# Another order inside a head group's four slots, and relative-position terms stored by blocks of 128 keys

## The chip, the cores and the metric

The kernel runs on one core of one Trainium2 chip. The metric is the device time of one execution in microseconds. Before the change it was 2924.61 us, the median of three runs (2921.96 to 2926.6).

## The reference

The input is x, 16 batches of 512 tokens with 256 features, and a conditioning vector for each batch. The block computes, all in 32-bit floats:

```
h = layernorm(x) * (1 + ca) + sa
q, k, v = h Wq + bq, h Wk + bk, h Wv + bv                 (16 heads of 16 features)
scores[l, r] = (q_l . k_r + q_l . pos[l - r] + k_r . pos[l - r]) / 4
ctx = softmax(scores) v
x = x + ga * layernorm(ctx Wo + bo + h)
h = layernorm(x) * (1 + cb) + sb
x = x + gb * (sum of the 2 of 8 experts that the router picks)
```

What matters here is the middle: each score has three terms. The one of q and k is called content. The two that use the table pos of relative distances are the q terms and the k terms.

## The kernel before

A prologue normalizes the batches and computes q, k and v, which go to DRAM (`prepare`, L261). It also brings q and k into a form in which the relative-position terms can be made by matmuls (`stationary`, L327).

The terms are made in 64 blocks. A block n covers 64 queries by 128 keys for 128 batch-heads. For one of its four parts, `q_set` (L156) runs 8 matmuls on TensorE into four PSUM banks, and ScalarE copies the four banks into an SBUF block `two[n % 2]` (L175). `k_set` (L177) runs 16 matmuls into four banks, and VectorE adds each bank to the block (L195). `store` (L199) writes a part to the DRAM tensors `rel_d`. The first ten blocks are made in the prologue (`blocks`, L375, LEAD = 10).

Then the main part works through 64 units. A unit is 128 queries of one batch, with four head groups of four heads. For a head group:

- `load_scores` (L577) brings the terms of its four heads from `rel_d` into a tile `s` of 128 x 4 x 512.
- `content` (L637) runs four 32-row matmuls into four banks. VectorE adds them to `s`, scales by 0.25 and takes each row's maximum (L650), then negates the maxima (L654).
- `exps` (L657): ScalarE's exponential of one head, in place.
- `turn` (L664): four transposes of one head's exponentials into one bank, and ScalarE's copy of it to SBUF (L671).
- `context` (L674): 16 matmuls in 32-column tiles form the weighted sum of v for the four heads, all from the copies of `turn`. It has a PSUM bank of its own.

The rest of a unit runs one unit later: `back`, `contextT`, `project` (L695 to L744), `residual` and `norm2` (L747, L756), where the reciprocal root of a variance is taken on GpSimd (L101), `modulate`, `route`, `mask_t` and `bias` (L768 to L821), and then four pairs of experts. `experts` (L823) runs two whole-array matmuls of 512 columns into one bank. `expert_sums` (L833) reads both halves of this bank: VectorE accumulates the first half (L838), ScalarE scales the second (L842), and GpSimd adds that up (L848). Term blocks run ten ahead of the units, four parts of q terms and four of k terms in a unit.

The order is written out by hand. Time is cut into slots, 16 for a unit and 4 for a head group, and `at(slot, order, fn, ...)` (L862) says in which slot and in which order a function issues its instructions; the loop at L910 calls them by slot and order. Every engine runs its own instructions in this order, and waits on semaphores for what it needs from the others. DMAs are issued by SP, in the same order.

All matmul outputs but the weighted sum come from one pool of seven PSUM banks (`bank`, L122). A matmul into a bank waits until the last reader of what the bank held is done.

In the four slots of a head group TensorE did, before the change: slot 0 a transposed head and content of the next group; slot 1 a transposed head and the weighted sum of the group before; slot 2 a transposed head, q terms and experts; slot 3 k terms and a transposed head, with the smaller pieces between. The change touches these lines:

```python
            at(q0 - 2, 7, exps, u, g, (0, 1))
            at(q0 - 1, 7, exps, u, g, (2, 3))
            at(q0 + 5, 4, context, u, g)
            at(z + 18 + 4 * pr, 6, experts, u, pr)
            at(z + 19 + 4 * pr, 1, expert_sums, u, pr)
                at(z + 2 + 4 * g, 4, rel.q_set, n, g)
                at(z + 15 + 4 * g, 2, rel.k_set, n, g)
```

## Time and profile before

| | us |
|---|---|
| median of three runs | 2924.61 |
| the profiled execution | 2935.72 |
| span of the profiled execution | 2934.0 |
| first transposed head of the first unit | 496.9 after the start |
| a unit in the steady part | 39.11 |
| TensorE, ScalarE, VectorE, GpSimd busy in the unit from 1494.0 to 1533.1 us | 39.10, 30.78, 26.41, 9.47 |
| share of the 16 DMA engines busy from 1000 to 2500 us | 0.91 |
| longest DMA entries by bytes: rel_d<-r, s<-rel_d | 256 issues of 1024 KB each, 8.5 and 7.8 us to landing |

A profile is one execution taken by the hardware profiler. Each engine's instructions have a start and a duration; for matmuls the end is modelled, so TensorE's busy time holds waits that fall between two matmuls of one group. The profiled execution is 11.1 us longer than the median of the runs.

### The profile page before, as it was taken

Reading aid. Unit: us, or ns where it says so; the run is one execution under the profiler, and the core shown is the slowest. Engines: PE = TensorE matmul, PEld = TensorE weight load, DVE = VectorE, ACT = ScalarE, POOL = GpSimd, SP = SyncE. Lnnn points to the kernel's source line nnn. Section 1 sums busy time; section 2 is a strip of 40 time slices with the busy share of each in tenths; the row PEclk is TensorE's granted clock in tenths of the full one; section 3 lists DMA queues with packets and bytes.
Section 4 is the critical chain, followed back from the end, with each engine's and each line's share of the span. In section 5 each row is a group of like instructions: output and inputs, shape, how many; then the busy total and the mean of one; then the engine's idle time right before and its main releaser. Section 6 shows DMA issues by size and latency. Waiting matters only on the chain.

```text
span 2934.0 us, 76492 instructions
## 1 busy us (share of the span) xinstructions
PE 2770.9 (94%) x30186; PEld 1803.2 (61%) x30186; DVE 1837.4 (63%) x5140; ACT 2068.8 (71%) x3938; POOL 630.1 (21%) x863
## 2 busy tenths in 40 slices
PE   8779963999999999999999999999999999999997
PEld 5556642666666666666666666666666666665654
DVE  5446542666666666666666666666666666675553
ACT  2345432877777777777777777777777777777774
POOL 1000000022222222222222222222222222223333
PEclk9989876999999999999999999999999999999998
DMA  6879998688988998899888998889899898897561
GB/s 181 306 253 317 296 299 273 223 276 283 286 282 277 294 307 279 274 285 292 281 278 286 291 289 281 278 285 288 278 286 307 279 286 281 278 278 264 201 238 43
DMA packets 855350, 796.49 MB, mean 271 GB/s; under 512 B 25545, under 2 KB 649409, under 8 KB 854737
## 3 DMA queue, kind: packets, MB, share of 16 engines
q1 hardware_dynamic: 854032, 790.03, 85.2%
q8 instruction: 240, 3.93, 0.5%
q10 hardware_dynamic: 960, 1.57, 0.2%
q14 instruction: 118, 0.96, 0.1%
HBM read 462.20 MB, written 328.25 MB: 269 GB/s over the span
## 4 chain that ended last, share of the span: by engine, by line
PE 77%; DMA 2%; POOL 2%; DVE 1%; SPq 1%; ACT 1%; issue 1%; POOLq 0%; DVEq 0%; ACTq 0%
PE pt L669 18%; PE fpy L827 15%; PE qk L644 12%; PE pq L165 10%; PE pc L684 8%; PE pk L186 8%; PE ph L732 2%; DMA vu<-v_d 1%; PE fpl L788 1%; PE pcl L699 1%; PE fpb L818 1%; PE fpt L775 1%; POOL qm L614 1%; PE pct L716 0%; POOL rstd L101 0%
## 5 line engine op out<-in xcount | busy, mean ns | idle before, releaser
L671 ACT COPY pT<-pt 128x512 f32<-128x512 f32 x1024 | 595.3, 584 | 317.9 <-PE pt L669 295.3
L195 DVE TENSOR_TENSOR r<-pk,r 128x512 f32<-128x512 f32 x1024 | 635.0, 683 | 189.2 <-PE pk L186 164.3
L660 ACT ACTIVATE s<-s,mx 128x512 f32<-128x512 f32 x1024 | 689.7, 731 | 43.3 <-DVE mx L654 39.7
L650 DVE CUSTOM_DVE_ANT_0 s<-qk,s 128x512 f32<-128x512 f32 x1024 | 644.1, 685 | 85.8 <-PE qk L644 81.4
L669 PE MATMUL pt<-ident,s 128*128 128x128 f32 x4096 | 660.0, 284 | 10.8 <-ACT s L660 10.4
L175 ACT COPY r<-pq 128x512 f32<-128x512 f32 x1024 | 525.6, 603 | 153.9 <-PE pq L165 137.1
L669 PEld LDWEIGHTS pt<-ident,s 128*128 128x128 f32 x4096 | 450.0, 143 | 284.7 <-ACT s L660 73.8
L827 PE MATMUL fpy<-we_sb,fhT 128*128 128x512 f32 x1024 | 506.1, 617 | 0.0
L848 POOL TENSOR_TENSOR ye<-ye,ye 128x256 f32<-128x256 f32 x192 | 140.5, 732 | 1597.4 <-ACT ye L842 1105.8
L838 DVE SCALAR_TENSOR_TENSOR fy<-fpy,fmask,fy 128x256 f32<-128x256 f32 x256 | 123.5, 482 | 471.6 <-PE fpy L827 319.3
L644 PE MATMUL qk<-k,qm 32*128 32x512 f32 x2048 | 380.1, 650 | 28.0 <-POOL qm L614 28.0
L186 PEld LDWEIGHTS pk<-t_f,ke 32*128 32x128 f32 x8192 | 268.3, 190 | 189.5 <-ACT r L175 124.1
L165 PE MATMUL pq<-t_r,qe 32*128 32x256 f32 x4096 | 370.5, 409 | 4.2 <-DMA qe<-eq_d 2.8
L186 PE MATMUL pk<-t_f,ke 32*128 32x128 f32 x8192 | 319.8, 287 | 8.8 <-DVE r L195 3.6
L827 PEld LDWEIGHTS fpy<-we_sb,fhT 128*128 128x128 f32 x1024 | 175.0, 190 | 195.2 <-issue 159.8
L165 PEld LDWEIGHTS pq<-t_r,qe 32*128 32x128 f32 x4096 | 240.2, 186 | 82.4 <-issue 41.7
L684 PE MATMUL pc<-pT,vu 128*32 128x128 f32 x8192 | 279.1, 277 | 0.0
L684 PEld LDWEIGHTS pc<-pT,vu 128*32 128x32 f32 x8192 | 209.9, 110 | 44.1 <-issue 43.5
L644 PEld LDWEIGHTS qk<-k,qm 32*128 32x128 f32 x2048 | 133.4, 184 | 101.5 <-DVE r L195 47.6
L101 POOL TENSOR_TENSOR rstd<-rstd,mhalf 128x1 f32<-128x1 f32 (+1 forms) x144 | 87.9, 610 | 436.0 <-DVE rstd L100 428.1
L842 ACT ACTIVATE ye<-fpy,fmask 128x256 f32<-128x256 f32 x256 | 125.3, 490 | 51.3 <-DVE fy L838 51.3
L614 POOL TENSOR_SCALAR qm<-qs,par 128x256 f32<-128x256 f32 x128 | 117.7, 932 | 150.1 <-DMA k<-k_d 137.8
(110 smaller groups left out, 2061.7 us busy)
## 6 DMA issues: line engine op xcount, KB each, us to landing
rel_d<-r SPq DMA_DIRECT2D x256, 1024.0 KB, 8.5
s<-rel_d SPq DMA_DIRECT2D x256, 1024.0 KB, 7.8
vu<-v_d SPq DMA_DIRECT2D x64, 576.0 KB, 7.5
ke<-ek_d SPq DMA_DIRECT2D x128, 256.0 KB, 7.2
k<-k_d SPq DMA_DIRECT2D x128, 256.0 KB, 6.6
gt<-gates_d SPq DMA_DIRECT2D x64, 256.0 KB, 4.7
v_d<-v SPq DMA_DIRECT2D x16, 576.0 KB, 6.4
xt<-in_x SPq DMA_DIRECT2D x16, 512.0 KB, 5.9
```

The costliest lines, as they stand in the source:

```text
L165: nc.tensor.matmul(bs[t][:, a * 256 : (a + 1) * 256], e[32 * t : 32 * t + 32, (g % 2) * 2 + a, :], t_r[32 * t : 32 * t + 32, :, m0 : m0 + RK],
L175: nc.scalar.copy(dst[:, t], bs[t].rearrange("p (a c) -> p a c", a=2))
L186: nc.tensor.matmul(bs[t][:, a * 128 : (a + 1) * 128], e[32 * t : 32 * t + 32, a, :], t_f[32 * t : 32 * t + 32, :, m0 : m0 + LQ], start=Tru ...
L195: nc.vector.tensor_tensor(dst, bs[t].rearrange("p (r l) -> p l r", r=8), dst, ALU.add)
L614: nc.gpsimd.tensor_scalar(qm[:, pa], qs, par[:, pa : pa + 1], None, ALU.mult)
L644: nc.tensor.matmul(bs[t], t_["q"][rows, pa, cc, :], t_["k", cc][rows, :], start=True, stop=True)
L650: nc.vector.tensor_tensor_reduce(st[:, t, :], bs[t], st[:, t, :], 0.25, -3.0e38, ALU.add, ALU.max, mx[:, t : t + 1],)
L660: nc.scalar.activation(t_["s", g][:, t, :], t_["s", g][:, t, :], AF.Exp, bias=t_["m", g][:, t : t + 1])
L669: nc.tensor.transpose(pt[:, cols], t_["s", g][:, t, cols], ident)
L671: nc.scalar.copy(pT, pt)
L684: nc.tensor.matmul(pc[32 * t : 32 * t + 32, g, :], t_["v"][:, rb, h * VW : h * VW + 32], pTs[t][:, rb * P : (rb + 1) * P], start=(rb == 0) ...
L827: nc.tensor.matmul(py, t_["hT"][:, kc, :], we_sb[:, kc, pr * 2 * E : (pr + 1) * 2 * E], start=(kc == 0), stop=(kc == NE - 1),)
```

## The change

In a head group the weighted sum is issued one slot earlier and so stands directly before content of the next group. Experts stay in their slot but now stand before the q terms. The sums over the experts (VectorE and ScalarE) move from the head of the following slot to directly behind the experts. Of the four exponentials one is issued in slot 2 and three in slot 3, where it was two and two. Q terms are copied in two halves: banks 0 and 1 directly after the matmuls, banks 2 and 3 in the next slot, after that slot's transposed head, which now stands before the k terms. `bias` is issued one slot later.

The DRAM tensors of the terms change their layout from (batch-head, query, 512 keys) to (batch-head, block of 128 keys, query, 128 keys). What a store writes for one head is now one contiguous piece of 16 x 128 numbers. A load reads pieces of 128 numbers, and is four DMAs, one for each head.

```diff
-    rel_d = [dram.tile([P, P, S], F32, tag=f"rel_{n}", name=f"rel_d{n}") for n in range(8)]
+    rel_d = [dram.tile([P, NL, P, RK], F32, tag=f"rel_{n}", name=f"rel_d{n}") for n in range(8)]
...
+            self.banks = bs
+            self.q_copy(n, g, (0, 1))
+
+        def q_copy(self, n, g, ts):
             dst = self.two[n % 2][:, 16 * g : 16 * g + 16, :].rearrange(
                 "p (a t i) r -> p t a (i r)", a=2, t=4
             )
-            for t in range(4):
-                nc.scalar.copy(dst[:, t], bs[t].rearrange("p (a c) -> p a c", a=2))
+            for t in ts:
+                nc.scalar.copy(dst[:, t], self.banks[t].rearrange("p (a c) -> p a c", a=2))
...
-                out=rel_d[s * 4 + lb][:, l0 : l0 + 16, rb * RK : (rb + 1) * RK],
+                out=rel_d[s * 4 + lb][:, rb, l0 : l0 + 16, :],
...
                 rel.q_set(n, g)
+                rel.q_copy(n, g, (2, 3))
...
-        nc.sync.dma_start(
-            out=st, in_=rel_d[s * 4 + lb][h0 : h0 + 7 : 2].rearrange("h l r -> l h r")
-        )
+        for t in range(4):
+            nc.sync.dma_start(
+                out=st[:, t, :].rearrange("p (rb r) -> p rb r", r=RK),
+                in_=rel_d[s * 4 + lb][h0 + 2 * t].rearrange("rb l r -> l rb r"),
+            )
...
-            at(q0 - 2, 7, exps, u, g, (0, 1))
-            at(q0 - 1, 7, exps, u, g, (2, 3))
+            at(q0 - 2, 6.3, exps, u, g, (0,))
+            at(q0 - 1, 5, exps, u, g, (1, 2, 3))
             for t in range(4):
                 at(q0 + t, 3, turn, u, g, t)
-            at(q0 + 5, 4, context, u, g)
+            at(q0 + 4, 4, context, u, g)
...
-        at(z + 16, 7, bias, u)
+        at(z + 17, 6, bias, u)
         for pr in range(4):
             at(z + 18 + 4 * pr, 6, experts, u, pr)
-            at(z + 19 + 4 * pr, 1, expert_sums, u, pr)
+            at(z + 18 + 4 * pr, 6.6, expert_sums, u, pr)
...
-                at(z + 2 + 4 * g, 4, rel.q_set, n, g)
-                at(z + 15 + 4 * g, 2, rel.k_set, n, g)
+                at(z + 2 + 4 * g, 7, rel.q_set, n, g)
+                at(z + 3 + 4 * g, 3.5, rel.q_copy, n, g, (2, 3))
+                at(z + 15 + 4 * g, 4, rel.k_set, n, g)
```

## The prediction

> **What bounds the kernel now.** I read the page first, then the busy time by stretches, then the timelines of TensorE, ScalarE and VectorE over one unit, then the waits.

> ```profile
> span 2934.0 us, 76492 instructions
> PE 2770.9 (94%) x30186; PEld 1803.2 (61%) x30186; DVE 1837.4 (63%) x5140; ACT 2068.8 (71%) x3938; POOL 630.1 (21%) x863
> ...
> PE   8779963999999999999999999999999999999997
> ...
> DMA  6879998688988998899888998889899898897561
> ```

> TensorE looks full from 600 us to the end, and a unit (16 slots, 4 head groups) takes 39.11 us from its first transpose to that of the next unit (1494.03 to 1533.15 us), every unit alike. But ends of matmuls are modelled, so a wait inside a group of matmuls counts as busy. I therefore read starts, from one group to the next. Timeline of TensorE in the third head group of a unit (start, duration, what):

> ```profile
> 1488.36 2.02 PE L165 MATMUL pq<-t_r,qe 32*128 32x256 f32 x16
> 1490.30 1.98 PE L827 MATMUL fpy<-we_sb,fhT 128*128 128x512 f32 x4
> 1492.21 1.17 PE L186 MATMUL pk<-t_f,ke 32*128 32x128 f32 x32
> 1493.32 0.66 PE L669 MATMUL pt<-ident,s 128*128 128x128 f32 x4
> ```

> The q terms take 1.94 us here, and 1.08 in another group of the same unit; 0.87 us of it is a wait for a PSUM bank. In the four groups of the unit from 1494 us the q terms take 1.08, 1.15, 1.26 and 1.95, and content 1.84, 0.96, 1.62 and 1.07 (0.96 where a 32-row matmul follows, 1.07 where a transpose does). So waits are 1.13 us in q terms and 1.32 in content: 2.45 of 39.11 us. The waits name who held the banks (window 800 to 2800 us):

> ```profile
> PEld qk L644 <- DVE r L195: 41.9, 187, 0.3
> ...
> ACT ye L842 <- DVE fy L838: 17.5, 26, 1.7
> ...
> PEld pq L165 <- DVE mx L650: 14.7, 46, 0.3
> ```

> Content waits for VectorE's adds on the k terms, q terms for its maxima over content. The totals are small because most of such a wait hides in a busy matmul; the pairs are what matters. The middle line matters below: ScalarE's half of an expert pair (L842) waits for VectorE's half (L838). The same third group on ScalarE and VectorE:

> ```profile
> 1489.99 2.05 ACT L175 COPY r<-pq 128x512 f32<-128x512 f32 x4 [0.89 <-PE pq L165]
> 1491.91 1.36 ACT L660 ACTIVATE s<-s,mx 128x512 f32<-128x512 f32 x2
> 1493.14 0.49 ACT L842 ACTIVATE ye<-fpy,fmask 128x256 f32<-128x256 f32 x1
> ```

> ```profile
> 1489.84 0.42 DVE L654 TENSOR_SCALAR mx<-mx 128x4 f32<-128x4 f32 x1
> 1490.17 0.41 DVE L760 BATCH_NORM_STATS2 stats<-x 128x6 f32<-128x256 f32 x1
> ...
> 1492.17 0.41 DVE L765 TENSOR_SCALAR xn<-x,mv,rstd 128x256 f32<-128x256 f32 x1 [1.18 <-POOL rstd L101]
> 1492.50 0.48 DVE L838 SCALAR_TENSOR_TENSOR fy<-fpy,fmask,fy 128x256 f32<-128x256 f32 x1
> ```

> In this group VectorE runs the second layer norm between the maxima and its expert half: 2.66 us from L654 to L838, of which 1.18 wait for GpSimd. Before the change that hurts nobody: ScalarE has made its four q copies and two exponentials before it comes to L842.

> [...] four transposes take 0.436 us between whole-array work and 0.530 ahead of tiled matmuls (0.094 more), and the first of the four expert matmuls takes 0.533 to the next start after q terms where the others take 0.429 (0.104 more). [...] Here, packets of 512 bytes took 29 ns on average, of 2048 bytes 97, of 8192 bytes 319.

> **The change, part by part.**

> *Weighted sum beside content, experts beside q terms.* Whole-array and tiled work alternate three times a group instead of four: 0.094 + 0.104 = 0.198 us a group, 0.79 a unit[...]. Also the sum (1.01 us) now stands between k terms and content, and experts (1.81) between content and q terms, which covers the 2.45 us of waits. At most 3.24 us a unit are to be gained.

> *ScalarE's new queue.* Its order in a group becomes: three transposed copies, exponential 0, L842, q copies 0 and 1, fourth transposed copy, q copies 2 and 3, exponentials 1 to 3. Now L842 stands ahead of the q copies. By the banks that the built program hands out, the third and fourth k-term banks are those of q copies 0 and 1, and one transpose group (0.59 us) stands between q terms and k terms.

> - Ordinary group, q terms ending at T: L842 is done about T + 0.14, the copies start 0.48 apart and last 0.59, so the second is out at T + 1.21, and 0.05 goes to the semaphore. The k terms go round their four banks, so nearly all of their 1.1 us follows: end T + 2.32. Without a wait it is T + 0.59 + 1.10 = T + 1.69. Added: 0.63, three times 1.9.
> - Third group, counted from the end of the second group's k terms: adds from 0.1, four by 0.60, then the first norm's statistics and L750 until 4.3; maxima 4 by 0.61, so L654 at 6.9; 2.66 on, L838: 9.5 to 10.0; L842 to 10.5; copies 0 and 1 out at 11.6; k terms end at 12.7. TensorE alone: projection 1.17, transposes 0.53, sum 1.01, content 1.2, transposes 0.93, experts 1.81, q terms 1.28 (0.2 of them a wait), transposes 0.59, k terms 1.10: 9.6. Added: 3.1, and the 0.2.
> - What is late next: ScalarE does exponentials 1 to 3 (0.61 each) only after the q copies, and small copies behind them hold banks that content takes. In the first group the mask's copy ends 4.68 after T, content would start at T + 4.13: 0.5. In the fourth the modulated copies end 1.1 after content could use them: 1.1.

> Sum of the unit: 39.11 − 2.45 − 0.79 + 1.9 + 3.3 + 1.6 = 42.67, so 42.6 us, +3.5. The same reckoning with the old order gives 39.2 against the 39.11 measured, so its steps are sound to some 0.1 where they can be tested.

> *The last ten units* have no q or k terms. The weighted sum there follows the fourth transposes with only one transpose group between, and that fourth copy stands behind L842: 0.5 to 0.9 us a group, less what runs hidden; I take +3 a unit (0 to 4.5).

> *Terms by 128 keys.* A store turns from 2048 packets of 512 bytes into 128 of 8192: 2048·29/16 = 3.7 us of the 16 DMA engines becomes 128·319/16 = 2.6. A load turns from 512 of 2048 bytes into 2048 of 512: 3.1 becomes 3.7. Four of each a unit: −2.0 us of some 36. In the steady part that is worth nothing, TensorE covers it. Loads are four DMAs instead of one: 12 more a unit at about 0.45 us on SP, 5.4 us. SP has room:

> ```profile
> SPq L203 <- DVE r L195: 442.6, 43, 11.2
> ```

> that is 10 us a unit in which the store at the head of SP's queue waited for VectorE (window 800 to 2500 us). A load is still issued eight slots, near 20 us, ahead of its content, and lands in 7.8; should that cover go, a load late by x costs x. In the prologue DMA is the bound from 350 to 490 us (share 0.83 to 1.09 in most stretches); 16 stores fall there, 16·1.1 = 18 us less transfer, not all on the path. I take −15 (0 to −40).

> Total: 2934.0 + 54·3.5 + 10·3 − 15 = 3138 us of span. The profiled execution took 2935.7, the median 2924.6 is 11.1 below: 3138 + 1.7 − 11.1 = **3129 us**.

> **Rivals.**

> *Cover works, queue does not bite* (not slower): all waits go and no new one comes: 2934.0 − 54·3.24 − 15 = 2744, so 2735 us. For it: the new neighbours do cover VectorE's work, and ScalarE has idle time (30.8 of 39.1 us busy). Against: the chain L765, L838, L842, copies, k terms. It decides once new waits stay below 3.24 us a unit, which needs L842 not to hold the copies in the third group.

> *Only the short wait* (about the same or faster): the third group costs 0.63 like the others and content waits stay at 0.5: 39.11 − 3.24 + 2.5 + 0.5 = 38.9 a unit, 2934 − 11 − 15, so 2899 us. For it: GpSimd may answer sooner. Against: 1.18 us waited in every unit of before.

> *Transfers become the bound* (slower): if reads of 512 bytes cost 40 ns, not 29, the loads take 20.5 us a unit, transfers near 39.5 and late loads show: with the queue's wait hidden behind that, 40 to 44 us a unit, near 3100 us. Against: 512-byte packets averaged 29 ns at a 0.91 share.

> **How the numbers follow.** The main case has 0.80, cover works 0.07, only the short wait 0.06, transfers 0.07. The main case by itself spans 3050 to 3200 (±1.2 us a unit, ±15 at the two ends); to leave no more than 2 in 10 out I reach down towards smaller third-group waits, 3010. A measurement of this kernel tells 0.2% from no change. Faster 0.12, same 0.01, slower 0.87.

> **What would show it.** Right: k terms at 1.7 us in three groups and above 3.5 in the third; L842 idle before it, released by L838; q terms near 1.08; content near 1.07 in the second and third groups; the unit at 42 to 43 us; the first weighted sum some 10 to 20 us earlier. Wrong: k terms at 1.10 in every group, or loads of s named as what content waits for.

## The result: 10% slower, and the profile after

The changed kernel takes 3217.6 us (median of four runs, 3202.4 to 3232.5), the kernel before 2925.6 in the same session: a ratio of 1.100, interval 1.094 to 1.105. The forecast was 3129 us, range 3010 to 3200. The direction and the place of the loss were as forecast; a tenth was lost where the sum had 7%.

The profiled execution took 3202.4 us, 1.7 of it outside the span. From the page of the changed kernel, its head, and two rows of the span in 40 slices (TensorE's busy tenths and the clock it was granted):

```profile
span 3200.7 us, 78389 instructions
...
PE 2955.9 (92%) x30186; PEld 1919.0 (60%) x30186; DVE 1841.2 (58%) x5140; ACT 2058.1 (64%) x3938; POOL 628.8 (20%) x863
...
PE   8789749999999999999999999999999999998887
...
PEclk9899859999999999999999999999999999999987
DMA  6977987878887878877778887788877778886661
```

VectorE and ScalarE are busy for about as long as before (1837 and 2069 us), and TensorE issues exactly as many instructions. No engine has more to do. TensorE's 185 us more of busy time are waits inside its matmul groups, and a slower clock, as the following views show. The DMA row is lower than before, and between 800 and 2500 us no TensorE instruction waits for a load of `s`.

The start of `contextT`'s transposes, one pair per unit, marks each unit; from one to the next is an interval, and the intervals divide the span without a gap. All numbers are of the two profiled executions:

| stretch | before, us | after, us | difference, us | forecast, us |
|---|---|---|---|---|
| start to the first of them | 541.3 | 522.8 | −18.5 | −15 |
| 53 intervals in the steady part | 2068.3 | 2309.3 | +241.0 | +189 |
| the ten intervals after | 290.0 | 333.0 | +43.0 | +30 |
| rest | 34.4 | 35.6 | +1.2 | 0 |

Before, every steady unit takes 39.11 us. After, one in five takes 42.80 us and nearly all others 43.90. The 42.80 is close to the forecast (42.6). The extra 1.1 us in four of five units was not in it.

The steps of the forecast are seen best in the third head group of a unit. Timeline of TensorE, changed kernel (start, duration, what, the wait before it in brackets; line numbers are those of the changed kernel: 4 higher than before for the k terms and the q copies, 7 higher behind them):

```profile
1489.44 1.88 PE L834 MATMUL fpy<-we_sb,fhT 128*128 128x512 f32 x4
1491.25 1.48 PE L165 MATMUL pq<-t_r,qe 32*128 32x256 f32 x16
1492.66 0.66 PE L676 MATMUL pt<-ident,s 128*128 128x128 f32 x4
1493.25 0.48 PE L190 MATMUL pk<-t_f,ke 32*128 32x128 f32 x2
1495.31 2.96 PE L190 MATMUL pk<-t_f,ke 32*128 32x128 f32 x30 [1.58 <-ACT ye L849]
1498.20 0.69 PE L782 MATMUL fpt<-ident,xn 128*128 128x128 f32 x2
```

Two of 32 matmul instructions of the k terms go out, then TensorE stands still until ScalarE's expert half (L849) is done. From start to start the group takes 4.95 us, where before it took 1.10. In a unit of 42.80 us it takes 4.09. The same stretch on ScalarE, and then on VectorE:

```profile
1491.79 0.72 ACT L667 ACTIVATE s<-s,mx 128x512 f32<-128x512 f32 x1 [1.46 <-DVE mx L661]
1494.78 0.47 ACT L849 ACTIVATE ye<-fpy,fmask 128x256 f32<-128x256 f32 x1 [2.27 <-DVE fy L845]
1495.15 1.06 ACT L179 COPY r<-pq 128x512 f32<-128x512 f32 x2
```

```profile
1491.58 0.17 DVE L661 TENSOR_SCALAR mx<-mx 128x4 f32<-128x4 f32 x1
1491.66 0.42 DVE L767 BATCH_NORM_STATS2 stats<-x 128x6 f32<-128x256 f32 x1
...
1493.94 0.41 DVE L772 TENSOR_SCALAR xn<-x,mv,rstd 128x256 f32<-128x256 f32 x1 [1.46 <-POOL rstd L101]
1494.27 0.48 DVE L845 SCALAR_TENSOR_TENSOR fy<-fpy,fmask,fy 128x256 f32<-128x256 f32 x1
```

This is the forecast chain, link by link: maxima, second norm with its wait for GpSimd, VectorE's expert half (L845), ScalarE's half (L849), and only then the q copies (L179), which start at 1495.15 us, 0.37 after L849, though the q terms end at 1492.73. From L661 to L845 it is 2.69 us, forecast 2.66. The k terms wait first for L849 itself, because one of their four banks is that of the expert pair, then for the q copies.

The waits of the changed kernel (800 to 2800 us; us in total, times, longest):

```profile
ACT ye L849 <- DVE fy L845: 190.9, 137, 2.3
...
PEld pk L190 <- ACT ye L849: 79.4, 46, 1.8
PE pk L190 <- ACT ye L849: 70.5, 45, 1.6
...
PEld pk L190 <- ACT r L179: 50.8, 265, 0.2
```

The first row was 17.5 us before, and the second and third rows did not exist. The two expert halves read the same bank; why ScalarE's waits for VectorE's was not shown.

What the forecast did not have is in the busy time by stretches. The columns are the stretch, then busy us and instructions of PE, PEld, DVE, ACT, POOL, then the granted clock, the DMA share and GB/s. The first row is from a unit of 42.80 us, the others from the next, right after the wait:

```profile
1451.00:1453.00 2.00, 0.51 (x3) 0.33 (x3) 0.81 (x2) 1.03 (x3) 0.57 (x2) 1.00 0.01 3
...
1496.00:1498.00 2.00, 2.00 (x28) 1.77 (x27) 0.11 (x1) 2.00 (x5) 0.06 (x1) 0.60 0.00 0
1498.00:1500.00 2.00, 2.00 (x20) 1.48 (x22) 2.00 (x4) 2.00 (x5) 0.00 (x0) 0.55 0.02 4
1500.00:1502.00 2.00, 2.00 (x42) 1.04 (x31) 0.51 (x2) 0.70 (x2) 0.00 (x0) 1.00 0.50 193
```

After the wait TensorE runs at half its clock from 1496.38 us for 3.41 us, then at full speed again. The 53 steady intervals hold 42 such stretches. Before, the clock stays at 1.00 from 525 us to 2655 us.

### The profile page after: what moved, and what is told of

Its sections match the earlier page's. It is cut to its first block, busy times and chain, and to the rows that moved or that the text cites. A ratio compares the mean times of both kernels' runs of the same rounds, so it can differ in the third digit from the quotient of the medians.

```text
span 3200.7 us, 78389 instructions
## 1 busy us (share of the span) xinstructions
PE 2955.9 (92%) x30186; PEld 1919.0 (60%) x30186; DVE 1841.2 (58%) x5140; ACT 2058.1 (64%) x3938; POOL 628.8 (20%) x863
## 3 DMA queue, kind: packets, MB, share of 16 engines
q10 hardware_dynamic: 960, 1.57, 0.1%
## 4 chain that ended last, share of the span: by engine, by line
PE 42%; POOL 10%; DMA 9%; issue 8%; DVE 6%; SPq 6%; ACT 5%; POOLq 0%; DVEq 0%; ACTq 0%
PE pk L190 8%; PE pt L676 8%; PE fpy L834 6%; PE qk L651 6%; PE pc L691 6%; SPq L588 4%; POOL qm L621 4%; PE pq L165 3%; DVE s L657 3%; DMA s<-rel_d 3%; DMA k<-k_d 2%; POOL rstd L101 2%; DMA rel_d<-r 2%; ACT s L667 2%; POOL x L760 1%
## 5 line engine op out<-in xcount | busy, mean ns | idle before, releaser
L676 PEld LDWEIGHTS pt<-ident,s 128*128 128x128 f32 x4096 | 472.1, 146 | 321.5 <-issue 170.3
L190 PE MATMUL pk<-t_f,ke 32*128 32x128 f32 x8192 | 530.1, 302 | 88.4 <-ACT ye L849 81.5
L179 ACT COPY r<-pq 128x512 f32<-128x512 f32 x1024 | 551.8, 608 | 40.1 <-PE pq L165 23.3
L190 PEld LDWEIGHTS pk<-t_f,ke 32*128 32x128 f32 x8192 | 406.8, 194 | 213.5 <-ACT ye L849 91.7
L651 PE MATMUL qk<-k,qm 32*128 32x512 f32 x2048 | 352.0, 664 | 23.2 <-DMA s<-rel_d 23.0
L165 PE MATMUL pq<-t_r,qe 32*128 32x256 f32 x4096 | 336.1, 406 | 4.2 <-DMA qe<-eq_d 2.9
L165 PEld LDWEIGHTS pq<-t_r,qe 32*128 32x128 f32 x4096 | 216.0, 186 | 195.6 <-issue 46.8
L691 PE MATMUL pc<-pT,vu 128*32 128x128 f32 x8192 | 317.0, 295 | 5.3 <-ACT pT L678 5.3
L849 ACT ACTIVATE ye<-fpy,fmask 128x256 f32<-128x256 f32 x256 | 121.4, 474 | 285.3 <-DVE fy L845 281.2
L691 PEld LDWEIGHTS pc<-pT,vu 128*32 128x32 f32 x8192 | 232.6, 118 | 66.0 <-issue 48.3
L101 POOL TENSOR_TENSOR rstd<-rstd,mhalf 128x1 f32<-128x1 f32 (+1 forms) x144 | 87.8, 609 | 585.2 <-DVE rstd L100 562.7
L845 DVE SCALAR_TENSOR_TENSOR fy<-fpy,fmask,fy 128x256 f32<-128x256 f32 x256 | 123.1, 481 | 129.7 <-PE fpy L834 129.7
L651 PEld LDWEIGHTS qk<-k,qm 32*128 32x128 f32 x2048 | 102.7, 192 | 108.6 <-issue 55.7
```

What stands on the lines that cost most here:

```text
L165: nc.tensor.matmul(bs[t][:, a * 256 : (a + 1) * 256], e[32 * t : 32 * t + 32, (g % 2) * 2 + a, :], t_r[32 * t : 32 * t + 32, :, m0 : m0 + RK],
L179: nc.scalar.copy(dst[:, t], self.banks[t].rearrange("p (a c) -> p a c", a=2))
L190: nc.tensor.matmul(bs[t][:, a * 128 : (a + 1) * 128], e[32 * t : 32 * t + 32, a, :], t_f[32 * t : 32 * t + 32, :, m0 : m0 + LQ], start=Tru ...
L651: nc.tensor.matmul(bs[t], t_["q"][rows, pa, cc, :], t_["k", cc][rows, :], start=True, stop=True)
L676: nc.tensor.transpose(pt[:, cols], t_["s", g][:, t, cols], ident)
L691: nc.tensor.matmul(pc[32 * t : 32 * t + 32, g, :], t_["v"][:, rb, h * VW : h * VW + 32], pTs[t][:, rb * P : (rb + 1) * P], start=(rb == 0) ...
```

## The experiments

Each kernel ran in three timed rounds beside the kernel before, which took between 2928.8 and 2933.2 us in these sessions. Ratios are to that. The table gives the mean steady interval (51 of them) and the mean of the first nine of the last ten, from each profile.

| kernel | time, us | ratio, interval | steady, us | last, us |
|---|---|---|---|---|
| before | 2925.6 | | 39.11 | 29.6 |
| changed | 3217.6 | 1.100 (1.094 to 1.105) | 43.70 | 33.8 |
| layout only | 2917.6 | 0.996 (0.994 to 0.998) | 39.11 | 29.5 |
| order only | 3229.5 | 1.104 (1.101 to 1.107) | 43.86 | 34.0 |
| norm behind the expert half | 3042.6 | 1.039 (1.037 to 1.040) | 40.68 | 34.2 |
| third pair's matmuls twice | 3146.2 | 1.074 (1.072 to 1.076) | 42.79 | 33.6 |
| half of it twice | 3195.6 | 1.091 (1.088 to 1.093) | 43.68 | 33.5 |
| a quarter of it twice | 3196.7 | 1.091 (1.089 to 1.094) | 43.70 | 33.6 |
| weighted sum moved only | 3054.2 | 1.042 (1.040 to 1.043) | 41.04 | 31.4 |
| q copies together | 3227.2 | 1.101 (1.099 to 1.103) | 44.03 | 34.0 |
| modulated copies a slot later | 3183.9 | 1.087 (1.084 to 1.090) | 43.37 | 34.2 |
| norm behind, projection first | 3001.8 | 1.024 (1.023 to 1.026) | 40.38 | 31.0 |
| new order repaired | 2908.7 | 0.992 (0.990 to 0.994) | 39.04 | 29.1 |
| old order mended | 2865.1 | 0.977 (0.975 to 0.979) | 38.19 | 28.8 |

### The two parts of the change apart

*Layout only.* To the kernel before, the three hunks on the terms' memory layout (the tile, the store, four loads for one), nothing else.

> The order of the kernel before, with only the terms' new layout and its four loads a group. Theory (all of the loss is in the order): units stay at 39.11 us, the first weighted sum comes about 16 us earlier (16 stores of the prologue at 2.6 instead of 3.7 us of the DMA engines), so about 2910 us (2900 to 2918). Rival (512-byte reads or twelve more loads on SP's queue bind the steady part): 40 us a unit or more, 2960 us and up. Third: the layout is hidden in the prologue too, 2925 us.

Measured 2917.6 us, and 39.11 us a unit. From the page of this kernel:

```profile
span 2915.5 us, 78452 instructions
...
PE 2767.3 (95%) x30186; PEld 1801.8 (62%) x30186; DVE 1839.5 (63%) x5140; ACT 2066.4 (71%) x3938; POOL 628.7 (22%) x863
```

The span is 18.5 us shorter than before, and the first unit's `contextT` comes at 526.2 instead of 541.3 us. The gain lies in the prologue. Twelve more DMAs a unit on SP and reads of 512 bytes cost nothing in the steady part. The rival of the transfers falls.

*Order only.* The changed kernel with those three hunks undone.

> The changed order with the old layout of the terms. Theory: everything of the loss is here, units of 42.8 and 43.9 us as in the changed kernel, prologue longer by 15 to 17 us: about 3233 us (3215 to 3250). Rival (the two parts bite only together, the new loads being late in the new order): units under 41 us, below 3080 us.

Measured 3229.5 us, units of 42.8 and 43.9 us, a few of 45. The layout has no part in the loss: it is all in the order.

### The third group's wait

*Norm behind the expert half.*

```diff
-        at(z + 10, 0, norm2, u)
+        at(z + 10, 6.8, norm2, u)
```

> The changed kernel with the second layer norm on VectorE moved behind the expert half of its group. Theory (the chain xn, fy, ye, q copies, k terms of the third group, and the half-speed clock that its wait sets off): the third group's k terms 1.7 us instead of 4.1 to 4.95, no half-speed window left, unit 42.8 - 2.4 = 40.4 us, 3217.6 - 54 x 3.3 = about 3040 us (3015 to 3065). Rival A (the half-speed windows come from the other waits, or from anything else): unit about 41.3, 3217.6 - 54 x 2.4 = 3088 us. Rival B (VectorE's work is merely late elsewhere: norm2 then holds something else up): unit 42 us or more, above 3120 us.

Measured 3042.6 us. The steady unit is 40.67 us, each one alike. The k terms of the third group, on TensorE's timeline of this kernel:

```profile
1470.67 2.05 PE L190 MATMUL pk<-t_f,ke 32*128 32x128 f32 x32
1472.65 0.44 PE L782 MATMUL fpt<-ident,xn 128*128 128x128 f32 x2
```

From start to start they take 1.98 us instead of 4.09 to 4.95, and no half-speed stretch is left in the steady part. One line's place in VectorE's queue was worth 175 us. The wait's own length is 112 of them (4.09 less 1.98 us, 53 times), and 48 are the clock, as the next experiment shows; the rest is about what the changed kernel's median lies above its profiled run. The chain from the norm to the k terms stands, and rivals A and B fall; the k terms keep 0.27 us more than the 1.71 of the other groups.

*Third pair's matmuls twice.* This asks whether the clock, and not the queue, makes the other 1.1 us. More work is put where TensorE waits:

```diff
-        for kc in range(NE):
-            nc.tensor.matmul(
...
+        for _ in range(2 if pr == 2 else 1):
+            for kc in range(NE):
+                nc.tensor.matmul(
...
```

> The changed kernel with the third expert pair's four matmuls run twice into the same bank (1.72 us more of TensorE work a unit, the same result). That work falls into the time in which the third group's k terms wait. Theory (the wait starves TensorE long enough that its clock is halved for one 3.4 us window): k terms of the third group 4.09 - 1.72 = 2.4 us, no half-speed windows, all units 42.8 us, so it is faster although it does more: 3217.6 - 54 x 0.9 + 10 x (0 to 1.7) = 3170 to 3190 us. Rival A (the clock drops for another reason): units 43.7 on average as before, 3217 to 3235 us. Rival B (the expert half waits for TensorE, not for the norm): 1.7 us a unit more, about 3310 us.

Measured 3146.2 us: 71 us faster with 256 more matmul instructions. TensorE's timeline in the third group of this kernel (L850 is L849 of the changed kernel):

```profile
1472.80 1.15 PE L165 MATMUL pq<-t_r,qe 32*128 32x256 f32 x16
1473.88 0.66 PE L676 MATMUL pt<-ident,s 128*128 128x128 f32 x4
1474.46 0.48 PE L190 MATMUL pk<-t_f,ke 32*128 32x128 f32 x2
1475.13 2.12 PE L190 MATMUL pk<-t_f,ke 32*128 32x128 f32 x30 [0.18 <-ACT ye L850]
```

The wait is still there, but short: the group takes 2.71 us. Every steady unit but one of 42.93 us takes 42.77 to 42.80 us; none takes 43.9. The granted clock by stretches is 1.00 in all of 1440 to 1472 us here, two of its rows:

```profile
1460.00:1464.00 4.00, 4.00 (x45) 2.29 (x47) 1.50 (x6) 3.17 (x7) 0.73 (x1) 1.00 0.67 197
1464.00:1468.00 4.00, 4.00 (x72) 3.09 (x66) 3.25 (x7) 3.47 (x7) 0.07 (x1) 1.00 0.95 279
```

So two kernels with the same queue, and with units of the same 42.80 us when the clock is whole, differ by 47.7 us over the 53 steady intervals (2261.6 against 2309.3). The one has 42 half-speed stretches in them and the other none. That is the price of the clock, some 1.1 us for each. Of the 71 us between the medians another 5 are in the last units, and 19 lie between the medians and the profiled runs (the changed kernel's median is 15.2 us above its own, this one's 4.0 below).

*Half and a quarter of it twice.* One matmul call more on all 512 columns, or on 256:

```diff
+        if pr == 2:
+            nc.tensor.matmul(
+                py, t_["hT"][:, 0, :], we_sb[:, 0, pr * 2 * E : (pr + 1) * 2 * E],
+                start=True, stop=True,
+            )
```

> The changed kernel with half of the third expert pair's matmuls run twice (0.86 us more of TensorE work a unit instead of 1.72, the same result). The third group's k terms then take 4.09 - 0.86 = 3.2 us, a wait of 2.1 us instead of 3.0 (1.3 with the whole pair). Theory (the half-speed windows come of the length of this wait): none left or few, units of 42.8 us, about 3150 us (3140 to 3170). Rival [...]: units of 43.9 us remain, 3200 us or more.

> The same with a quarter of the pair's matmuls (0.43 us more of TensorE work, the same result): the third group's k terms take about 3.65 us, a wait of 2.55 us. Theory (length of the wait, and where it falls in the fixed raster of 3.41 us windows): half-speed windows in fewer units than 4 of 5, say 2 of 5, so about 3175 us (3150 to 3205). Rival (a threshold on the wait alone, above 2.55): none, 3147 us. Rival (below 2.55): as without it, 3200 to 3235 us.

Measured 3195.6 and 3196.7 us: both theories of mine on the length missed, and the rival that a shorter wait is enough holds, with times 3 to 4 us below what it gave. With the quarter 10 of 51 steady units take 42.8 us, with the half 13, and nearly all others 43.9 or more, as without the extra work. The 21 to 22 us that both gain are not in the steady part (43.7 us a unit as before): 5 are in the last units, and most of the rest is that the changed kernel's median lies 15 us above its profiled run. With the half, in a unit whose clock was whole during the k terms (L854 is L849 of the changed kernel):

```profile
1491.49 0.48 PE L190 MATMUL pk<-t_f,ke 32*128 32x128 f32 x2
1492.99 2.12 PE L190 MATMUL pk<-t_f,ke 32*128 32x128 f32 x30 [1.02 <-ACT ye L854]
```

The group takes 3.54 us, not 3.2: 0.33 us of the extra work went into the q terms' own wait for a bank (1.41 us there falls to 1.08). By starts, the longest stillness within the k terms is 1.82 us in the changed kernel, 1.72 with a quarter, 1.29 with the half, 0.45 with the whole pair. The first three kernels have their clock halved in most units, the last in none of the steady ones.

### The other terms of the sum

*Weighted sum moved only.* To the kernel before:

```diff
-            at(q0 + 5, 4, context, u, g)
+            at(q0 + 4, 4, context, u, g)
```

> The kernel before, with only the weighted sum moved one slot on, next to content; nothing else of the change. Theory (in the old place it stands between content and the q terms, so it covers the q terms' wait for VectorE's maxima; taken away from there the wait shows): q terms 1.9 to 2.3 us in all four groups instead of 1.08 to 1.95, content without its waits of 0.9 and 0.7 us, unit 39.11 + 1.9 = 41 us, tail units some 3 us longer: 2926 + 54 x 1.9 + 10 x 3 = about 3055 us (3030 to 3080). Rival (the neighbours save a mode change a group, nothing else moves): unit 38.7 us, 2905 us.

Measured 3054.2 us. TensorE's timeline (this kernel's lines are those of before):

```profile
1494.58 1.14 PE L644 MATMUL qk<-k,qm 32*128 32x512 f32 x8
1495.65 1.09 PE L669 MATMUL pt<-ident,s 128*128 128x128 f32 x8
1496.68 2.17 PE L165 MATMUL pq<-t_r,qe 32*128 32x256 f32 x16
```

Content takes at most 1.07 us, its waits are gone. The q terms take 2.10 to 2.49 us, and they wait for the maxima: in the waits between 800 and 2500 us, TensorE's loads for q terms behind the maxima (L650) go from 13.7 to this:

```profile
PEld pq L165 <- DVE mx L650: 106.3, 373, 0.3
```

Call cover what TensorE does between a group of matmuls and the next group that takes the same banks, while the other engines empty them. Here cover was moved from one taker of banks to another: over the unit the q terms take 9.2 us instead of 5.4, content 4.2 instead of 5.5. The change as a whole avoids this loss with the experts in front of the q terms, and then it is the k terms that stand uncovered.

*q copies together.*

```diff
-                at(z + 3 + 4 * g, 3.5, rel.q_copy, n, g, (2, 3))
+                at(z + 2 + 4 * g, 7.1, rel.q_copy, n, g, (2, 3))
```

> The changed kernel with the four q copies in one go before the fourth transposes (the halving undone). Theory (the k terms wait for q copies 0 and 1 only, which stay where they are): k terms 1.71 us in three groups and over 4 in the third as before, 3217 us within 15. Rival (the halves are what makes things late: ScalarE's two late copies hold the banks of the next content or the next q terms): two thirds of a us a group or more comes back, below 3100 us. Other way (the fourth transposed copy, now behind all four, holds up the weighted sum): 3250 us or more.

Measured 3227.2 us, no gain. Its steady units with a whole clock take 42.75 to 42.78 us against 42.80, so the halves neither help nor hurt. In the middle of its profile units of 43.9 and 44.85 us alternate: two half-speed stretches in a unit.

*Modulated copies a slot later.*

```diff
-        at(z + 11, 6, modulate, u)
+        at(z + 12, 6, modulate, u)
```

> The changed kernel with the second norm's transposes and their modulated copies one slot later, nothing else. Theory (the fourth group's content waits 1.1 us for the modulated copies' bank; in the last ten units the transposes wait 3.8 us for the norm): content of the fourth group 1.1 instead of 2.15 us, but the router's matmuls then wait 0.7 us for the copies, so 0.3 us a unit; in the last ten units 1 to 3 us each: 3217.6 - 54 x 0.3 - 10 x 2 = about 3180 us (3150 to 3205). Rival (the term counts in full): below 3150 us. Rival (it moves nothing, all waits pass to other places): 3217 us.

Measured 3183.9 us. The total is the forecast's, and its parts are not. The fourth group's content falls from 2.15 to 1.42 us in a unit with a whole clock, the router's matmuls take 0.59 instead of 0.37, and the unit is 42.23: 0.57 us less, not 0.3. The last units gain nothing (34.2 us against 33.8), where 1 to 3 us each were expected. Two units in three now hold a half-speed stretch, at 1.5 us each. The term of 1.1 us for this content was real in the changed kernel, but only half of it could be had back.

*Norm behind, projection first.* The last units are still 4.7 us longer than before in the kernel with the norm moved. There, VectorE's statistics of the projection wait for ScalarE's copy of it, which stands behind the three late exponentials. On top of that kernel:

```diff
-        at(z + 7, 6, project, u)
+        at(z + 7, 4.7, project, u)
```

> The kernel with the norm behind the expert half (the quiet one of the earlier runs, 3042.6 us, 34.0 to 34.9 us for each of the last units), and the projection moved ahead of the three exponentials of its slot, so that ScalarE's copy of it no longer stands behind them; on TensorE nothing changes place. Theory for the last ten units (the projection's statistics wait 3.2 us for that copy, where before it was 1.5, and the second norm and its transposes wait with them): the steady unit stays at 40.67 us, the last ones fall by 1.4 to 2 us each, 3042.6 - 14 to 20 = about 3025 us. Rival (the last units are held by VectorE's maxima over content, or by the weighted sum's wait for the fourth copy): no change, 3042 us; or the late exponentials hold up the transposes, 3050 us.

The statistics in one of the last units, first with the norm moved alone, then with the projection first:

```profile
2886.59 0.43 DVE L748 BATCH_NORM_STATS2 stats<-ph 128x6 f32<-128x256 f32 x1 [3.18 <-ACT x L745]
```

```profile
2819.68 0.43 DVE L748 BATCH_NORM_STATS2 stats<-ph 128x6 f32<-128x256 f32 x1 [1.52 <-ACT x L745]
```

Measured 3001.8 us, 23 less than expected. The steady unit falls by 0.3 us, where no change was expected. The ten last intervals fall from 335.0 to 302.8 us, 3.2 a unit and more than the 1.4 to 2 expected: with the norm 1.7 us earlier, the third group's weighted sum (1.64 to 1.01 us) and content (2.02 to 1.07) lose their waits too. Before the change this wait is 1.52 us as well. The clock takes part here too: the ten intervals hold 13 times 3.41 us at half speed with the norm moved alone and none with the projection first. How much of the 3.2 us is the wait and how much the clock was not separated.

### Two mended orders

*New order repaired.*

```diff
-        at(z + 7, 6, project, u)
+        at(z + 7, 2, project, u)
-        at(z + 10, 0, norm2, u)
-        at(z + 11, 6, modulate, u)
+        at(z + 11, 0, norm2, u)
+        at(z + 12, 6, modulate, u)
-        at(z + 17, 6, bias, u)
+        at(z + 17, 2, bias, u)
-                at(z + 3 + 4 * g, 3.5, rel.q_copy, n, g, (2, 3))
-                at(z + 15 + 4 * g, 4, rel.k_set, n, g)
+                at(z + 2 + 4 * g, 7.1, rel.q_copy, n, g, (2, 3))
+                at(z + 15 + 4 * g, 2, rel.k_set, n, g)
```

> The changed kernel with what was found late moved: second norm and modulated transposes one slot later, projection and bias before the transposes of their slot, q copies together, k terms before the fourth transposes. Theory (third group's wait, half-speed windows and content's waits for small copies go; a wait of 0.7 us for the q copies stays in every group's k terms, because experts no longer stand between q terms and k terms): unit 39.6 us, tail units 30 us, 3217.6 - 54 x 4.1 - 10 x 4.2 = about 2955 us (2930 to 2985), level with the kernel before or a little over it. Rival (the new order is good once the norm is out of the way): unit 38.3 us or less, below 2885 us.

Measured 2908.7 us, 46 less than I expected. The k terms take 1.92 to 2.11 us in three groups but 1.10 in the first, where the projection (1.26 us) now stands between q and k terms: there, cover came back. The steady unit, 39.04, is level with before, so the gain of 0.8% is the prologue and the last units.

*Old order mended.* To the kernel before, the new layout and two moves:

```diff
-                at(z + 2 + 4 * g, 4, rel.q_set, n, g)
+                at(z + 2 + 4 * g, 2, rel.q_set, n, g)
-        at(z + 11, 6, modulate, u)
+        at(z + 12, 6, modulate, u)
```

> The order of the kernel before with the new layout, and two steps moved: q terms stand before the third transposes of their slot instead of after them, so transposes and experts both stand between q terms and k terms; the second norm's transposes one slot later, so that their small copies no longer hold the bank of the fourth group's content. Theory (what counts is how much TensorE work stands between a group of four banks filled and the next taker of these banks): unit 39.11 - 0.86 = 38.25 us, 2917.6 - 54 x 0.86 = about 2871 us (2855 to 2895). Rival (the wait merely moves to the q terms, which come sooner after content): unit 39.1 us or more, 2915 us and up.

Measured 2865.1 us, 2.3% below the kernel before and the least of all kernels here. TensorE's timeline in one group of it (here the lines between L586 and the end are 2 higher than before):

```profile
1498.39 1.08 PE L686 MATMUL pc<-pT,vu 128*32 128x128 f32 x32
...
1499.94 1.35 PE L165 MATMUL pq<-t_r,qe 32*128 32x256 f32 x16
1501.22 0.66 PE L671 MATMUL pt<-ident,s 128*128 128x128 f32 x4
1501.71 1.88 PE L829 MATMUL fpy<-we_sb,fhT 128*128 128x512 f32 x4
1503.52 1.17 PE L186 MATMUL pk<-t_f,ke 32*128 32x128 f32 x32
```

The time is as expected, but the reason I gave was not the main one. Per unit, against the layout alone, by starts: the transposes take 8.31 instead of 8.72 us, the experts 7.25 instead of 7.66, content 5.12 instead of 5.49, the q terms 5.68 instead of 5.44. The first two, 0.82 of the 0.93 us, fit the alternation between tiled and whole-array work, three times a group instead of four, since the q terms now follow the weighted sum: 0.10 us a group in each, as the forecast priced them (0.79 in all). Content and the q terms, where the waits are, fall by only 0.13 together. The gain meant by the change was there, and this order takes it without uncovering anyone.

## Why the prediction was right in direction and short in size

- *Waits removed and mode changes saved.* Three alternations of tiled and whole-array work (mode changes) for four save 0.82 us a unit, forecast 0.79 (measured in the mended old order). That the weighted sum next to content costs nothing more was an estimate of mine, and the changed kernel fits with it: the sum takes 1.01 us and content behind it 1.07 in the second and third groups, as long as before where neither waits.
- *k terms in ordinary groups.* Forecast 1.69 us, measured 1.71.
- *k terms in the third group.* Forecast 1.10 + 3.1, measured 4.09 with a whole clock. The forecast named only the q copies' banks; there the expert pair's bank comes first, as the waits for L849 show. That the norm sets this off is shown by moving it.
- *What is late next.* Content 1.73 us in the first group and 2.15 in the fourth, forecast 0.5 and 1.1 over 1.07. Its removal gave back 0.57 of the 1.1, since other waits took the rest.
- *The unit.* Forecast 42.6 (its terms add to 42.67), measured 42.80 with a whole clock. **The step that failed is the sum of the unit**, which took each matmul at the duration it has before. After the third group's wait the clock is halved for 3.41 us in four of five units, and each such stretch costs 1.1 us, 47.7 us over the steady part. I had worked out that TensorE would stand idle for 3 us and did not ask what an idle TensorE does to its clock; that term was put at nothing without a reason. Without it the changed kernel would have taken some 3170 us (an estimate: 3217.6 less 47.7). The steady part of the kernel before shows no slower clock, but its prologue does. Between 450 and 475 us TensorE is busy for 7.92 of 25 us, and the granted clock is 0.50 (columns as above):

```profile
450.00:475.00 25.00, 7.92 (x80) 6.73 (x80) 6.94 (x10) 2.34 (x4) 0.00 (x0) 0.50 0.67 216
```

- *The last ten units.* Forecast +30, measured +43.0. The term was mis-sized: I looked at the weighted sum behind L849 and not at ScalarE's copy of the projection behind the late exponentials, which is worth 3.2 us a unit where the projection is put first. These ten intervals hold 14 times 3.41 us at half speed, against 4 before, and how much of the 13 us that cost is open.
- *The prologue.* Forecast −15, measured −18.5 in the profile, and 2917.6 against 2928.8 us for the layout alone.
- *From the profiled execution to the median.* I took the 11.1 us by which the median of before lies below its profiled run. Here the profiled run was the fastest of the four, 15.2 us below the median: 26.3 us of the miss. The four runs' mean granted clocks, 0.947, 0.939, 0.931 and 0.941, stand in the order of their times, 3202, 3222, 3232 and 3213 us. From 0.947 to 0.931 is some 31 half-speed stretches of 3.41 us more, and at 1.1 us each 34 us, where the times differ by 30 (an estimate from these clocks). So the spread fits with more half-speed stretches in the longer runs; only the shortest has a trace, so this is argued, not shown.

The miss of 89 us is 52 in the steady part (48 of it the clock), 13 in the last units, 26 of this offset, less 2 in the prologue and the rest.

Of the rivals: "cover works" needed ScalarE's expert half (L849 after) not to hold the copies; it holds them. "Only the short wait" needed a third group like the others; it is 2.4 us longer. "Transfers" is refuted by the layout alone.

## What to carry to other kernels

Work that covers the emptying of banks is not free to move: list, for every group of matmuls, how much TensorE work stands between it and the group that had its banks before, and check each taker that loses its cover, as the q terms did with the weighted sum (9.2 us a unit instead of 5.4) and the k terms with the experts (1.71 us a group instead of 1.10). Before an instruction is put ahead of others in an engine's queue, follow what it waits for in the one group that differs from the rest. And the wait of TensorE in the third group had two prices here, its length (112 us) and the slower clock after it (48 us); work put into the wait, even useless work, can pay, as the pair run twice shows (48 us in the steady part).

## What the runs showed of the hardware beyond the expected

A stillness of 1.29 to 1.85 us between two starts of TensorE, once in a unit of 43 us, was followed by 3.41 us at half clock in most units; with 0.45 us the clock stayed whole. No two starts in the steady part of the changed kernel lie more than 1.85 us apart.

The length of the stillness alone does not decide: in the nine units it is 1.82 to 1.85 us, as in the others, and the old order mended has a single stillness of 1.57 us, at 2560.7 us, with no half speed after it. What decides beside the length was not shown.
